# A fused depthwise convolution, MLP and gate on one core: the last 16 channels in eight PSUM banks, a reordered first product group, and image 2's forms on VectorE

## The chip, the cores and the metric

The kernel runs on one core of a Trainium2 chip. TensorE multiplies matrices into PSUM; VectorE (DVE), ScalarE (ACT) and GpSimd (POOL) work elementwise; SyncE (SP) mostly issues transfers. The metric is the device time of one execution in microseconds. Everything is float32.

## The reference, cut to what matters

The input is 32 images of 384 channels and 28 x 28 pixels.

```python
residual = x                                               # (32, 384, 28, 28)
y = conv(x, dw_w, padding=3, groups=384) + dw_b            # depthwise, 7 x 7
y = to_nhwc(y)
mu, var = mean(y, -1), mean((y - mu) ** 2, -1)             # over the channels of a pixel
y = (y - mu) * rsqrt(var + 1e-6) * ln_g + ln_b
y = gelu(y @ w1 + b1)                                      # 384 -> 1536
gx = sqrt(sum(y ** 2, pixels))                             # per image and channel
nx = gx / (mean(gx, -1) + 1e-6)
y = grn_g * (y * nx) + grn_b + y
x = residual + to_nchw(y @ w2 + b2)                        # 1536 -> 384
# gate: mean, max and min over the pixels of each channel, small products
logits = concat(avg @ W1.T, maxes * W2_2, min @ W3.T) @ Wfc.T
out = sigmoid(logits[:, :, None, None] + x)
```

The statistics of a pixel need all 384 channels. No image can therefore be normalized before the convolution of the last channel is done.

## The kernel before, in words

**Stage 1, the convolution.** Images lie in 8 groups of 4; a transfer `load_x` brings 32 channels of one group. `pad_x` copies it to a padded tile (POOL line 479, ACT line 481), and `turn_x` transposes it on TensorE (line 491) and copies it out of PSUM into `xt`. The first eight (padding, transposes) run one after the other before the first product. The 7 x 7 filter becomes banded 128 x 128 matrices `tmat`, loaded by `load_t` from the DRAM tables `fs`, which are built from `dw_w`. The channels go in 48 groups of 8 (s = 0 to 47). `conv` does two channels at a time: three matmuls each (lines 696, 698, 700), a transpose on VectorE (line 703) into `yt`, a sum over channels into `acc` (line 711), squares on ACT (line 717) and their sum into `ssum` on POOL (line 727). `yt` is stored to `yd` in DRAM. During these groups `form_w` (lines 556 to 573) writes combinations of w1 and w2 to `u1d` and `u2d`.

**The last 16 channels.** Groups 46 and 47 are done in two halves, first images 0 to 15, then 16 to 31, on four PSUM banks in turn (`pcs`). After the first half, image 0's last channels are read back (`load_y_part`), and its statistics are formed by `finish` in tiles (`late_tiles`) that lie where an `xt` tile was: sums, a VectorE reduction of the four partial square sums (line 746), a root on ACT (line 753), a reciprocal (line 754) and a store to `rsd[0]`; then the same for the other half into `rsd[1]`.

**Image 0.** `first_image` makes the raw image (line 789 VectorE, line 792 ACT), and `forms_up` the ten FORMS (line 358): sums and differences of channel blocks and pixel halves, named p to z. Since the first linear layer needs no statistics apart from a scale per pixel, image 0's products start on raw data, and `stretch` (line 952) multiplies the outputs by that scale afterwards. Later images are normalized first: `normed` (line 315) takes the loaded image `yi` and the broadcast scale `rb`.

**Stage 2, per image.** `up(b)` computes the first linear layer as four tiles t, in two pairs; each pair runs through 15 UPSTEPS, one matmul a tile and step (line 986, 128 x 392), so 60 in all. Results collect in banks A, B and C of a tile and are taken out by ACT copies (line 993) and VectorE sums (lines 997 to 1005). Weights come in groups of five steps by `load_u1` into six buffers in `ws`. `down(b)` computes the second layer in 38 STEPS of three matmuls (line 1116, 128 x 196) in banks A to I, whose operands are made by 39 SUMS on POOL (`sums`, line 1077); VectorE adds the products to the residual (lines 1132, 1134) and takes max and min (line 1143). Between them lie `gelu` (line 945), `square` into `junk` (line 958), `grn` (lines 1008 to 1025, with the one-column product `pg`), `scale` (lines 324 VectorE, 326 ACT) and `gate_store` (line 1160 on, with the product `pa` and its reading into `lt`).

**The order.** The driver runs up(0), up(1), down(0), up(2), down(1), up(3) and so on. `within(b)` and `beside(b)` are tables of hooks: at step (pair, matmul) of `up`, or at step i of `down`, they issue the elementwise work of neighbouring images. Instructions pinned by `keep_in_program_order` stay as written; the rest is ordered by a scheduler. All loads of stage 2 go through SP's queue. Every PSUM tile of stage 2 comes from one pool of eight buffers:

```python
    psz = ctx.enter_context(tc.tile_pool(name="psz", bufs=8, space=bass.MemoryType.PSUM))

    def bank(name):
        return psz.tile([P, 512], F32, tag="pz", name=name)
```

Of the kernel before, what the change touches and what calls it, by code (L numbers as in the profile page):

```python
# [13 lines left out]
P = 128  # L14
# [72 lines left out]
)  # L87
NS = len(UPSTEPS)
KT = FB // 3
# [108 lines left out]
def convnext_gate_kernel(  # L198
# [24 lines left out]
    rsd = [dram.tile([P, YR], F32, name=f"rsd_{i}") for i in range(2)]  # L223
# [18 lines left out]
    fct = const.tile([P, CB, NQ, R], F32, name="fct")  # L242
    eps_t = const.tile([P, 1], F32, name="eps_t")
# [9 lines left out]
    def load_u1(t, i):  # L253
        n = len(u1_tiles) % NU1
        w = ws[:, n * UG * P : (n + 1) * UG * P].rearrange("p (g c) -> p g c", c=P)
        nc.sync.dma_start(w, u1d[t, :, i : i + UG, :])
        u1_tiles.append(w)
        return w
# [12 lines left out]
    last_u2 = []  # L271
    B0 = min(B, 16)

    def load_y(b):
        yi = yis[b] = yip.tile([P, CB, NQD, YR], F32, tag="yi", name=f"yi_{b}")

        with tc.issue_after(last_u2[-1]) if last_u2 else ExitStack():
            for cb in range(CB):
                load_y_part(b, yi, cb, 0, P)
        load_rb(b)  # L280

    def load_rb(b):
        if b == 0:
            rb = d_room[:, : NQD * YR].rearrange("p (q n) -> p q n", n=YR)
        else:
            rb = rbp.tile([P, NQD, YR], F32, tag="rb", name=f"rb_{b}")
        rbs[b] = rb
        base = rsd[0 if b < B0 else 1]
        nc.sync.dma_start(
            rb,  # L290
            bass.AP(
                tensor=base.tensor,
                offset=base.offset + b * YR,
                ap=[[0, P], [B * YR, NQD], [1, YR]],
            ),
        )

    def load_y_part(b, yi, cb, p0, p1):
        nc.sync.dma_start(
# [8 lines left out]
    def normed(b, cbs=range(CB)):  # L308
# [5 lines left out]
        for cb in cbs:  # L314
# [4 lines left out]
            if b == 1:  # L319
# [8 lines left out]
    def forms_up(b, eng=nc.gpsimd, early=None):  # L328

        if b in feats:  # L330
            o, af = feats[b], early_af.pop()
            make_forms(b, eng, o, af, [d for d in FORMS if d[0] not in EARLY])
            return
        acc = accs.pop(b)
        o = feats[b] = {
            f"{k}{'ab'[h]}": acc[:, k, h * NH : (h + 1) * NH] for k in range(CB) for h in range(2)
        }
        ns = len(FORMS) - 1
        if b == 1:

            n = -(-ns * NH // (KD * NQ4))
            reserved.extend(slots[SLOTS - n :])
            del slots[SLOTS - n :]
            aft = d_room[:, (SLOTS - n) * KD * NQ4 :]
            af = [aft[:, n * NH : (n + 1) * NH] for n in range(ns)]
        else:
            af = [room_af[:, n, :] for n in range(ns)]
        if early:
            early_af.append(af)
        make_forms(b, eng, o, af, [d for d in FORMS if not early or d[0] in EARLY])  # L350

    EARLY, early_af = ("q", "t", "u"), []

    def make_forms(b, eng, o, af, todo):
        places = [d[0] for d in FORMS if d[0] != "w"]
        for name, place, in0, in1, op in todo:
            d = o[place] if name == "w" else af[places.index(name)]
# [4 lines left out]
    with ExitStack() as one:  # L362
# [8 lines left out]
        finp = one.enter_context(tc.tile_pool(name="finp", bufs=1))  # L371
# [18 lines left out]

        dww = scratch([CB, 49])
        nc.sync.dma_start(dww, dw_w.rearrange("(cb p) t -> p cb t", p=P))
# [49 lines left out]
        NX = C // XC  # L442
        NG = B // NB
        NXI = 8
        xi_last = tp.tile([P, NT], F32, name="xi_last")
        ssum = finp.tile([P, SQ, YR], F32, name="ssum")
        acc = finp.tile([P, 2, N], F32, name="acc")
        dws = finp.tile([P, 1], F32, name="dws")
        lr = tp.tile([P, CB, 2], F32, name="lr")
        mcol = tp.tile([P, FB], F32, name="mcol")  # L450
        for t in (ssum, acc):
            nc.gpsimd.memset(t, 0.0)
        GT = NX * NG
        xis = {}

        def load_x(i):

            k, g = divmod(i, NG)
            n = i % NXI
            t = xis[i] = xi_last if n == NXI - 1 else room[:, n * NT : (n + 1) * NT]  # L460
            base = x[g * NB, k * XC : k * XC + 1, :]
            nc.sync.dma_start(
                t,
                bass.AP(
# [817 lines left out]
    if B > 1:  # L1282
        load_y(1)
# [49 lines left out]
```

## Time and profile before

| what | us |
|---|---|
| median of three runs | 3053.81 (3052.74 to 3055.58) |
| the profiled execution | 3053.83 |
| its span | 3052.1 |
| TensorE busy in the span | 2998.0 |
| convolution ends, `up(0)` begins | 498.6, 504.85 |
| `up(1)` begins, `pg` of image 0 | 558.66, 582.47 |
| `down(0)` begins, ends | 604.64, 650.84 |
| from image to image afterwards | 78.2 |

Times inside the span start at its first instruction. The page gives busy time of each engine over the span; the windows give the same for stretches of it; the timeline lists what an engine did, with the idle time ahead of a line and what ended it. TensorE's own clock can be lowered: the windows list the share that was granted.

### The profile page before, as it was taken

Reading aid. Unit: us, or ns where it says so; the run is one execution under the profiler, and the core shown is the slowest. Engines: PE = TensorE matmul, PEld = TensorE weight load, DVE = VectorE, ACT = ScalarE, POOL = GpSimd, SP = SyncE. Lnnn points to the kernel's source line nnn. Section 1 sums busy time; section 2 is a strip of 40 time slices with the busy share of each in tenths; the row PEclk is TensorE's granted clock in tenths of the full one; section 3 lists DMA queues with packets and bytes.
Section 4 is the critical chain, followed back from the end, with each engine's and each line's share of the span. In section 5 each row is a group of like instructions: output and inputs, shape, how many; then the busy total and the mean of one; then the engine's idle time right before and its main releaser. Section 6 shows DMA issues by size and latency. Waiting matters only on the chain.

```text
span 3052.1 us, 43990 instructions
## 1 busy us (share of the span) xinstructions
PE 2998.0 (98%) x14436; PEld 2426.9 (80%) x14436; DVE 2042.5 (67%) x4643; ACT 1794.6 (59%) x2919; POOL 2444.9 (80%) x1819
## 2 busy tenths in 40 slices
PE   8999998999999999999999999999999999999998
PEld 8999996577777777777777777777777777777777
DVE  6767667756666666666666666666666666666665
ACT  4455553746666666666666666666666666666661
POOL 3457874699888888888888888888888888888897
PEclk9999999999999999999999999999999999999999
DMA  9899997445666566666666566666566566666545
GB/s 368 327 354 381 363 339 232 141 161 199 205 206 202 202 206 206 198 206 206 201 202 202 190 201 206 200 197 195 195 197 198 197 201 203 201 201 201 195 152 197
DMA packets 279369, 674.15 MB, mean 221 GB/s; under 512 B 24346, under 2 KB 99944, under 8 KB 273128
## 3 DMA queue, kind: packets, MB, share of 16 engines
q1 hardware_dynamic: 266456, 633.37, 61.6%
q10 hardware_dynamic: 12688, 37.97, 3.2%
q8 instruction: 118, 1.93, 0.2%
q14 instruction: 107, 0.88, 0.1%
HBM read 575.57 MB, written 95.68 MB: 220 GB/s over the span
## 4 chain that ended last, share of the span: by engine, by line
PE 89%; POOL 5%; DVE 4%; issue 1%; ACT 1%; DMA 1%; SPq 0%; DVEq 0%; ACTq 0%; POOLq 0%
PE ph_C L986 13%; PE ph_A L986 12%; PE ph_B L986 11%; PE pz_A L1116 8%; PE pz_C L1116 8%; PE pz_F L1116 7%; PE pz_D L1116 7%; PE pc L696 5%; PE pc L698 4%; PE pc L700 4%; PE pt L491 2%; PE pz_H L1116 2%; PE pz_I L1116 2%; PE pz_E L1116 2%; POOL d_room L1077 2%; DVE room L315 2%
## 5 line engine op out<-in xcount | busy, mean ns | idle before, releaser
L326 ACT ACTIVATE y<-y,vecs,gsc 128x784 f32<-128x784 f32 x372 | 359.1, 1031 | 463.9 <-DVE gsc L1024 463.9
L1077 POOL TENSOR_TENSOR d_room<-y 128x588 f32<-128x588 f32 x253 | 364.7, 1443 | 287.8 <-PE pz_B L1116 192.1
L945 ACT ACTIVATE y<-y,b1f 128x784 f32<-128x784 f32 x384 | 350.5, 945 | 209.1 <-DVE y L1003 179.0
L986 PE MATMUL ph_B<-room,ws 128*128 128x392 f32 x1240 | 461.7, 495 | 10.5 <-issue 6.0
L986 PE MATMUL ph_C<-room,ws 128*128 128x392 f32 x1240 | 462.0, 495 | 7.3 <-DVE y L1001 4.6
L986 PE MATMUL ph_A<-room,ws 128*128 128x392 f32 x1240 | 459.0, 492 | 3.4 <-ACT te L993 1.8
L1077 POOL TENSOR_TENSOR d_room<-d_room,y 128x588 f32<-128x588 f32 x308 | 441.3, 1437 | 16.8
L986 PEld LDWEIGHTS ph_C<-room,ws 128*128 128x128 f32 x1240 | 233.3, 190 | 191.3 <-DVE y L1001 28.7
L986 PEld LDWEIGHTS ph_A<-room,ws 128*128 128x128 f32 x1240 | 235.4, 190 | 177.0 <-ACT te L993 2.4
L986 PEld LDWEIGHTS ph_B<-room,ws 128*128 128x128 f32 x1240 | 235.6, 191 | 175.7 <-issue 6.8
L727 POOL TENSOR_TENSOR ssum<-ssum,sq 128x896 f32<-128x896 f32 x96 | 200.8, 2092 | 168.5 <-ACT sq L717 167.0
L958 ACT ACTIVATE junk<-y 128x784 f32<-128x784 f32 x384 | 329.1, 857 | 9.0
L1077 POOL TENSOR_TENSOR d_room<-y,d_room 128x588 f32<-128x588 f32 x214 | 306.4, 1438 | 26.7 <-PE pz_D L1116 15.7
L358 POOL TENSOR_TENSOR room<-room 128x392 f32<-128x392 f32 x303 | 303.9, 1020 | 11.9
L717 ACT ACTIVATE sq<-yt,dwb 128x224 f32<-128x224 f32 x376 | 160.4, 474 | 225.1 <-DVE yt L703 213.0
L1077 POOL TENSOR_TENSOR y<-y 128x588 f32<-128x588 f32 x180 | 259.0, 1439 | 7.1
L999 DVE TENSOR_TENSOR y<-y,ph_B 128x392 f32<-128x392 f32 x256 | 137.4, 557 | 158.3 <-ACT y L945 123.4
L997 DVE TENSOR_TENSOR y<-y,ph_C 128x392 f32<-128x392 f32 x384 | 213.1, 562 | 25.2
L703 DVE STREAM_TRANSPOSE yt<-pc 128x448 f32<-128x448 f32 x184 | 119.4, 649 | 136.9 <-PE pc L700 100.3
L1116 PE MATMUL pz_A<-d_room,u 128*128 128x196 f32 x1050 | 203.7, 330 | 0.1
L696 PE MATMUL pc<-xt,tmat 128*128 128x224 f32 x736 | 200.2, 354 | 0.6 <-ACT xt L502 0.6
L1116 PEld LDWEIGHTS pz_A<-d_room,u 128*128 128x128 f32 x1050 | 179.7, 191 | 7.7 <-POOL d_room L1077 0.4
(266 smaller groups left out, 6375.7 us busy)
## 6 DMA issues: line engine op xcount, KB each, us to landing
u<-u2d SPq DMA_DIRECT2D x487, 384.0 KB, 3.7
ws<-u1d SPq DMA_DIRECT2D x384, 320.0 KB, 3.0
tmat<-fs SPq DMA_DIRECT2D x47, 1420.0 KB, 10.8
ws<-u2d SPq DMA_DIRECT2D x121, 384.0 KB, 3.9
yi<-yd SPq DMA_DIRECT2D x95, 448.0 KB, 6.3
yd<-yt SPq DMA_DIRECT2D x47, 896.0 KB, 6.8
x<-in_x SPq DMA_DIRECT2D x32, 1176.0 KB, 5.6
out<-x ACTq DMA_DIRECT2D x31, 1176.0 KB, 9.6
```

The lines of the kernel that those rows point to most:

```text
L326: eng.activation(out, in_, AF.Identity, bias=add, scale=mul)
L358: tc.keep_in_program_order(eng.tensor_tensor(d, o[in0], o[in1], op))
L696: keep(nc.tensor.matmul(po, t[:, c, P : 2 * P], xc, start=True, stop=False))
L717: nc.scalar.activation(sq[:, cy % SQ + ci], yt[:, cy + ci], AF.Square, bias=dwb[:, cc + ci : cc + ci + 1], scale=1.0,)
L727: nc.gpsimd.tensor_tensor(to, base, sq, ALU.add)
L945: ins = nc.scalar.activation(y, y, AF.Gelu, bias=b1f[:, f : f + 1], scale=1.0)
L958: ins = nc.scalar.activation(junk, ys[b][:, f, :], AF.Square, accum_out=ssqs[b][:, f : f + 1])
L986: nc.tensor.matmul(banks[t, bk][:, :NH], wts[t][:, i % UG, :], o[opnd], start=(first == 1), stop=True, skip_group_check=True,)
L997: nc.vector.tensor_tensor(d, d, p, ALU.add)
L999: nc.vector.tensor_tensor(d, d, p, ALU.subtract)
L1077: nc.gpsimd.tensor_tensor(d[0], o[a][0], o[c][0], ALU.add if sign == "+" else ALU.subtract)
L1116: nc.tensor.matmul(pz[:, :NQ4], wt[:, i % UD, t, :], o[opnd][0][:, t, :], start=(first and t == 0), stop=(t == KD - 1), skip_group_check=True,
```

## The change

At the start, the image loads are issued before the load of `dw_w`, which becomes the third, and the pads run three image groups ahead of the transposes.

For the last 16 channels, eight PSUM banks (three of the transposes, one of the weight preparation, four of the convolution) hold one pair of channels each, and are filled by the two halves of images in turn. The first half only transposes its products out; sums and squares are taken once, over all images, in the second half. There is one `finish`, cut into four parts: part 0 (two POOL additions of the partial square sums, then forms v, x, z) before `up(0)`, and parts 1 to 3 from hooks in its first pair. `acc` and `ssum` move to a tile `stats` that stays; `rsd` is one tile.

The raw third block of image 0 is all ACT's. Its forms are POOL's: q, t, u, w early, p, r, s during the second half, v, x, z in part 0. The first pair of tiles of `up(0)` takes its steps in the order FIRST_UP, with a fourth bank D. The weights of the second pair, groups 0 and 1, are loaded early into four of the u2 buffers.

PSUM of stage 2 comes from two pools of four, taken in turn by four tiles. The two y buffers have a pool each, so that y_0 no longer lies over the tiles of the statistics; `junk` goes, and squares are written to `stats` or `room`.

Hooks of the first images move: `normed(1)`, forms and loads of image 2 go into the second pair of `up(0)`, stretches are all POOL's, half of image 0's later squares and five of its twelve scales are VectorE's, three of its sums (s1, s5, s6) too, and image 2's ten forms run on VectorE during `down(0)`.

The core of the diff ("..." marks what is left out):

```diff
+FIRST_UP = (
+    ("w", "A", 1, (("A", "copy", "E"),)),
+    ("1a", "B", 1, (("B", "rsub", "E"),)),
+    ("0b", "A", 0, (("A", "negated", "1b"),)),
+    ("0a", "B", 0, (("B", "negated", "0a"),)),
+    ("t", "C", 1, (("C", "add", "E"),)),
+    ("q", "A", 0, (("A", "plus", "0b"),)),
+    ("u", "B", 0, (("B", "minus", "1a"),)),
+    ("p", "D", 1, (("D", "copy", "2b"),)),
+    ("s", "C", 1, (("C", "add", "0a"),)),
+    ("x", "A", 1, (("A", "copy", "2a"),)),
+    ("r", "D", 0, (("D", "sub", "2a"), ("D", "sub", "0a"), ("D", "add", "0b"))),
+    ("2a", "C", 0, (("C", "add", "2a"),)),
+    ("v", "A", 0, (("A", "sub", "2b"), ("A", "sub", "1b"), ("A", "add", "1a"))),
+    ("z", "C", 1, (("C", "add", "2b"), ("C", "add", "1b"))),
+    ("2b", "D", 1, (("D", "add", "2b"),)),
+)
...
+PLACE = {step[0]: i for i, step in enumerate(UPSTEPS)}
...
-    rsd = [dram.tile([P, YR], F32, name=f"rsd_{i}") for i in range(2)]
+    rsd = dram.tile([P, YR], F32, name="rsd")
...
+    stats = const.tile([P, SQ * YR + 2 * NJ * B], F32, name="stats")
+    ssum = stats[:, : SQ * YR].rearrange("p (c n) -> p c n", n=YR)
+    acc = stats[:, SQ * YR :].rearrange("p (c n) -> p c n", c=2)
...
-        dww = scratch([CB, 49])
-        nc.sync.dma_start(dww, dw_w.rearrange("(cb p) t -> p cb t", p=P))
...
+        LENT = (3, 5, 7)
+        AHEAD = B // NB
...
+        dww = scratch([CB, 49])
+        for i in range(AHEAD):
+            load_x(i)
+            if i == 1:
+                nc.sync.dma_start(dww, dw_w.rearrange("(cb p) t -> p cb t", p=P))
...
-        for i in range(AHEAD):
-            load_x(i)
+        for i in range(NPAD):
+            pad_x(i)
         xt = new_xt(0)
         for i in range(NG):
-            pad_x(i)
...
+            if i + NPAD < NG:
+                pad_x(i + NPAD)
...
-                pc = pcs.pop(0)
-                pcs.append(pc)
+                pc = pcs[(s - NK + 2) * PAIRS + c2]
...
+            if b1 < B:
+                return
+            keep(nc.vector.tensor_tensor(acc, acc, pc[:, :, :N], ALU.add))
...
-                to, base = ssum, ssum
-                if nb < B and not b0:
-                    to = late["s2"]
-                    base = ssum if s == NK - 2 and cy < SQ else to
-                nc.gpsimd.tensor_tensor(to, base, sq, ALU.add)
+                ins = nc.gpsimd.tensor_tensor(ssum, ssum, sq, ALU.add)
+                if s >= NK - 2:
+                    keep(ins)
...
+                for i in range(2 * PAIRS):
+                    if i < 3:
+                        pc = psx.tile([P, 4, P], F32, tag="pt", name=f"pc_x{i}")
+                    elif i == 3:
+                        pc = psb.tile([P, 4, P], F32, tag="pb", name="pc_b")
+                    else:
+                        pc = psc.tile([P, 2, 256], F32, tag="pc", name=f"pc_c{i}")
+                    if i < 4:
+                        pc = pc.rearrange("p a b -> p (a b)").rearrange("p (c m) -> p c m", c=2)
+                    pcs.append(pc)
+                    if B0 < B:
+                        nc.vector.memset(
+                            pc[:, :, :N].rearrange("p c (j b) -> p c j b", b=B)[:, :, :, B0:],
+                            0.0,
+                        )
+                for i in (UG, 2 * UG, 0):
+                    for t in range(2):
+                        first_u1[t, i // UG] = load_u1(t, i)
...
-                            if not half:
-                                nc.sync.dma_start(yd[:, ch, :], y2[i])
-                            else:
-                                for q in range(NQD):
-                                    (nc.sync, nc.scalar)[q % 2].dma_start(
-                                        yd[q * B + b0 : q * B + b1, ch, :],
-                                        y2[i][q * B + b0 : q * B + b1],
-                                    )
+                            keep(nc.sync.dma_start(yd[:, ch, :], y2[i]))
+                        if b1 == B and n == PAIRS:
+                            first_image(2)
+                        if b1 == B and n == PAIRS + 1:
...
-    psz = ctx.enter_context(tc.tile_pool(name="psz", bufs=8, space=bass.MemoryType.PSUM))
+    pszs = [
+        ctx.enter_context(tc.tile_pool(name=f"psz{i}", bufs=4, space=bass.MemoryType.PSUM))
+        for i in range(2)
+    ]
+    nbanks = 0
 
     def bank(name):
-        return psz.tile([P, 512], F32, tag="pz", name=name)
+        nonlocal nbanks
+        nbanks += 1
+        return pszs[(nbanks - 1) // 4 % 2].tile([P, 512], F32, tag="pz", name=name)
...
+            steps = [(x[0],) + x[2:] for x in UPSTEPS]
+            if b == 0 and t2 == 0:
+                steps = FIRST_UP
+            for i, (opnd, bk, first, acts) in enumerate(steps):
                 for t in (t2, t2 + 1):
-                    if i % UG == 0:
-                        wts[t] = first_u1.pop((t, i), None) or load_u1(t, i)
+                    g, gi = divmod(PLACE[opnd], UG)
+                    if (t, g) not in wts:
+                        wts[t, g] = first_u1.pop((t, g), None) or load_u1(t, g * UG, b <= 1)
                     if i == 0:
...
+    def finish(part):
+
+        keep = tc.keep_in_program_order
+        tmp = yis[0].rearrange("p k q n -> p (k q n)")
+        mu0, s1, mu, va, s2, rs = (tmp[:, i * YR : (i + 1) * YR] for i in range(6))
+        if part == 1:
+            keep(nc.vector.tensor_tensor(mu0, acc[:, 0], acc[:, 1], ALU.add))
+            keep(nc.vector.transpose(s1, mu0))
+            keep(nc.vector.tensor_scalar(mu, s1, dws, 1.0 / C, ALU.add, ALU.mult))
+            keep(nc.vector.tensor_tensor(va, mu, mu, ALU.mult))
+        elif part == 0:
+            for n in (SQ // 2, 1):
+                to = ssum[:, :n] if n > 1 else s2.unsqueeze(1)
+                keep(nc.gpsimd.tensor_tensor(to, ssum[:, :n], ssum[:, n : 2 * n], ALU.add))
+            forms_up(0, ("v", "x", "z"))
+        elif part == 2:
+            keep(nc.vector.scalar_tensor_tensor(va, s2, 1.0 / C, va, ALU.mult, ALU.subtract))
+            keep(nc.vector.tensor_scalar(va, va, 0.0, EPS, ALU.max, ALU.add))
+            keep(nc.scalar.activation(s2, va, AF.Sqrt))
+        else:
+            keep(nc.vector.reciprocal(rs, s2))
+            keep(nc.sync.dma_start(rsd, rs))
+            load_rb(0)
+            if B > 1:
+                load_y(1)
...
+    LENT_SUMS = ("s1", "s5", "s6")
...
+            eng = nc.vector if b == 0 and name in LENT_SUMS else nc.gpsimd
...
+            at((0, 3), finish, 1)
+            at((0, 13), finish, 2)
+            at((0, 17), finish, 3)
+            for i, m in enumerate(first_outs[:HF]):
+                at((0, 29), stretch, m, nc.gpsimd)
+                at((2, 5 + 4 * i), gelu, b, m)
+                at((2, 7 + 4 * i), square, b, m)
             if B > 1:
-                at((0, 20), normed, 1)
-                at((0, 24), forms_up, 1)
-            for m in range(HF):
-                at((2, 4 * m), stretch, m, nc.gpsimd)
+                for cb in range(CB):
+                    at((2, 7 + 4 * cb), normed, 1, (cb,))
+                at((2, 16), forms_up, 1)
             if B > 2:
-                at((2, 0), load_y, 2)
+                at((2, 20), load_y, 2)
         elif b == 1:
-            for m in range(HF):
-                at((0, 2 * m), stretch, HF + m, (V, nc.gpsimd)[m % 2])
-                at((0, 6 + 2 * m), gelu, p, HF + m)
-                at((0, 17 + m), square, p, HF + m)
-            at((0, 23), grn, p)
+            for i, m in enumerate(first_outs[HF:]):
+                at((0, 2 * i), stretch, m, nc.gpsimd)
+                at((0, 6 + 3 * i), gelu, p, m)
+                if i % 2:
+                    at((0, 8 + 3 * i), square, p, m)
+                else:
+                    at((0, 11 + 3 * i), square, p, m, V)
+            at((0, 29), grn, p)
             for i, f in enumerate(order):
-                at((0, 24) if i < 6 else (2, 0), scale, p, f, V if i % 3 else A)
-            at((0, 26), sums, p)
-            at((2, 0), sums, p)
-            at((2, 12), sums, p)
+                at((2, 2 + i), scale, p, f, V if i in (1, 3, 5, 8, 11) else A)
+            for i in range(4, 30, 2):
+                at((2, i), sums, p)
...
-            at("after sums", forms_up, b + 2)
+            if b == 0:
+                for i, d in enumerate(FORMS):
+                    at(12 + 2 * i, forms_up, 2, (d[0],), V)
+            else:
+                at("after sums", forms_up, b + 2)
...
+    for g in EARLY_G:
+        for t in (2, 3):
+            w = u2_tiles[2 * g + t - 2][:, : UG * P].rearrange("p (g c) -> p g c", c=P)
+            tc.keep_in_program_order(
+                nc.sync.dma_start(w, u1d[t, :, g * UG : (g + 1) * UG, :])
+            )
+            first_u1[t, g] = w
+    finish(0)
     up(0, within(0))
     load_x(0)
```

## The prediction

> **What bounds the kernel now.** I read the page's busy shares first, then the chain that ended last, then the busy time by stage, then the idle times of TensorE in order of time.
>
> ```profile
> span 3052.1 us, 43990 instructions
> PE 2998.0 (98%) x14436; PEld 2426.9 (80%) x14436; DVE 2042.5 (67%) x4643; ACT 1794.6 (59%) x2919; POOL 2444.9 (80%) x1819
> PE 89%; POOL 5%; DVE 4%; issue 1%; ACT 1%; DMA 1%; SPq 0%; DVEq 0%; ACTq 0%; POOLq 0%
> ```
>
> TensorE is busy for 98% and carries 89% of the chain. No other engine can be the bound over the whole span; only TensorE's 54 us of idleness, and what it runs at a lower clock, can be won. The busy time by stage says where these lie:
>
> ```profile
> core 0: us, PE busy (x) PEld busy (x) DVE busy (x) ACT busy (x) POOL busy (x), PEclk, DMA share, GB/s
> 0.00:25.00 25.00, 13.74 (x85) 11.79 (x86) 9.64 (x20) 10.67 (x18) 7.16 (x21) 1.00 0.92 348
> 500.00:550.00 50.00, 35.82 (x97) 19.42 (x98) 33.37 (x56) 13.71 (x27) 18.99 (x15) 0.90 0.70 205
> 620.00:640.00 20.00, 16.52 (x85) 15.23 (x84) 8.94 (x25) 4.47 (x5) 19.45 (x14) 0.91 0.39 120
> 760.00:3000.00 2240.00, 2234.42 (x10129) 1752.34 (x10128) 1497.75 (x3563) 1383.72 (x2138) 1903.36 (x1433) 1.00 0.61 200
> 3000.00:3053.00 53.00, 39.22 (x221) 37.69 (x219) 27.10 (x99) 5.25 (x6) 32.92 (x26) 0.92 0.48 158
> ```
>
> Columns: window, length, busy time of each engine, granted clock. Idle TensorE: 11.3 us at the start, 14.2 between 500 and 550, 3.5 in the first `down`, only 5.6 in 2240 us of steady state, 13.8 at the end. The timeline of TensorE names the stalls of the transition; the last line is ScalarE's:
>
> ```profile
> 504.85 2.95 PE L986 MATMUL ph_B<-room,ws 128*128 128x392 f32 x4 [6.04 <-issue]
> 518.54 2.98 PE L986 MATMUL ph_B<-room,ws 128*128 128x392 f32 x4 [4.43 <-ACT y L993]
> 582.47 0.38 PE L1016 MATMUL pg<-gs,ones_f 128*128 128x1 f32 x2 [2.13 <-DVE gs L1014]
> 624.17 1.26 PE L1116 MATMUL pz_E<-y,u 128*128 128x196 f32 x6 [1.66 <-POOL y L1077]
> 634.14 2.24 PE L1116 MATMUL pz_H<-d_room,u 128*128 128x196 f32 x6 [1.52 <-POOL d_room L1077]
> 517.99 0.89 ACT L993 ACTIVATE y<-ph_B 128x392 f32<-128x392 f32 x2 [8.41 <-DMA rsd<-xt]
> ```
>
> Columns: start, length, work, and in brackets the idle time ahead and its releaser. The convolution ends at 498.6, `up(0)` begins at 504.85 after the forms, stops at 514.1 because ScalarE's first eviction waits for the store of the statistics, and `down(0)` ends at 650.84, held by POOL's `sums`.
>
> **What the Trainium skill says.** "TensorE: Matmul & The Clock Gate", What's actually happening: the clock is granted by recent activity, about 3.4 us of work bring it back. The trace agrees: after the two long waits four matmuls took 2.95 and 2.98 us, where four otherwise take 1.48. "SBUF — State Buffer", Who interferes with whom: a VectorE operation on two SBUF inputs and a POOL operation that reads SBUF exclude each other. The trace agrees: `normed` (line 315, 784 columns) took 0.97 us each in the three at 531, and 2.10 beside POOL's stretches at 550. "Perfetto Trace Analysis", Matmuls: matmul groups should rotate through PSUM banks so that eviction overlaps the next group. That is what the split into two pools of four touches; before, TensorE lost nothing to it in steady state.
>
> **The change part by part**, in the time base of the kernel before, against its profiled 3053.83 us (median of the runs 3053.81, so the two are one).
>
> *Start.* The first image loads are issued ahead of the `dw_w` load and the pads run three groups ahead, so the three ACT waits of 1.32 us between transposes go; the transposes could end near 17. The convolution then waits for the first half of `tmat_0` (8.5 us before); its source, the `fs` store, needs `dw_w`, which is now the third load, about 1 us later: first product near 17.8 instead of 20.42, a gain of 2.6. `tmat_1` (10.2 us, issued behind it) is then late: needed at 28.1, landing near 28.9, minus 0.9. Net 1.7; bounds 0 (all of it waits for `tmat`) and 3.
>
> *Last 16 channels.* Eight banks take away the one wait of 0.47 us on `acc` at 488.53; the first half loses 8 sums of 0.3 us on VectorE, 16 squares and 4 POOL adds, none on TensorE's path. Gain 0.5: convolution ends at 498.1.
>
> *Start of `up(0)`.* The reordered first group begins with w, 1a, 0b, 0a, t, q, u, which need only channel blocks 0 and 1 of the raw image, there by 498. So the 6.04 us go. Then 0b waits about 1.1 us, because ACT's copies of the w products sit behind the last squares (0.42 each) and the raw block. The y tiles no longer overlay the statistics, so the 4.43 go too, and with them 2 x 1.5 us of slow clock. A pair of tiles is 15 steps of two matmuls (1.32 us a step): 30 x 0.658 = 19.7. With 1.1 and 0.8 for the later forms, p, r, s and v, x, z, on POOL (1.02 each) the first pair ends near 519.7.
>
> *Statistics.* Two POOL adds replace two VectorE reductions of 1.7 us. Folds end near 508.7, the root and reciprocal (1.55) near 513.2, the store lands 3 us later, the broadcast of rs for image 0 near 521.7, image 1's loads near 525. Stretches (1.94 each) run 521.8 to 533.5, `normed(1)` 525 to 531, or to 534 if it contends with them. forms(1) start near 534, as before.
>
> *Second pair of `up(0)`.* 19.7 of matmuls. Groups 0 and 1 of the weights are early, in the u2 buffers. Group 2 of t=3 is an ordinary load; on SP's queue it stands behind image 2's three loads and its broadcast, and these wait for the buffers that `normed(1)` frees. Issue near 533 to 536, 7.8 us to land behind such loads: TensorE stalls 3.5 us and then runs slow for 1.4. Another 1.8 us go to evictions on VectorE queued behind `normed`. End near 546.1.
>
> *`up(1)`, then `down(0)`.* Half of `up(1)`, 19.7, and 2 us of waits as seen there before: pg near 567.8 instead of 582.47, so 14.7 earlier. After pg, `down(0)` hangs on POOL: ACT's and VectorE's scales let s2 start at +9.2; three sums moved to VectorE leave 28 up to s31, at 1.46 each 40.9; s31 releases the last 15 steps, 15 x 0.995 plus waits, 16.7. End at pg + 66.8 = 634.6; before 582.47 + 68.4 = 650.84. So 16.2 earlier. TensorE's own work would allow about 620.
>
> *Image 2's forms on VectorE.* They run under `down(0)`'s products, 10 x 0.5 us; POOL's 10.4 us at 644.5 go, and a wait of 0.36 us at 654.
>
> *Steady state.* Same instructions. But two pools of four change who shares a bank. In most images the new neighbour was read well before: F of `down`, read last (at 2217.37 when `up` began at 2215.09), is wanted again by the fifth matmul at 2217.72, 0.25 us to spare. In one image of four, from image 2 on, the gate's bank `pa` takes the bank of D, and its matmul and the first I step move near the end of `down`. VectorE then reads I behind a max and a min (0.92 each), the second I step waits some 0.3 us, and the evictions of the next `up` begin about 1.2 us later, past a slack near 1.2. I take 0.5 us for each of 7 images, 3.5 us of loss; bounds 0 and 8.
>
> The end (13.8 us idle) has nothing changed in it. **Sum:** 1.7 + 0.5 + 16.2 + 0.4 - 3.5 = 15.3; 3053.8 - 15.3 = 3038.5, taken as 3038.
>
> **The rivals.** *TensorE-bound:* the weights of the second pair arrive in time and the sums keep ahead, as the early groups and three sums on VectorE suggest; against it, POOL was 19.45 of 20 us busy in 620 to 640. `down(0)` would end near 623, 11 us earlier than I say: 3027. *Queue:* image 2's loads hold SP longer, since `normed(1)` contends with the stretches (2.62 at worst in 550 to 566), group 2 of both tiles of the pair comes late, and pg falls near 575: 7 us of the gain lost, 3045. *No gain in the sums:* pg earlier, but VectorE's forms and sums exclude POOL's, each sum 2.0 instead of 1.46: 28 x 0.54 = 15, all of it; the start and forms remain, less the bank waits: 3052. *Slower:* the bank of F in every image. If VectorE reads F a microsecond later than before, the fifth matmul waits 0.75 us, and evictions behind it as much again; over 31 images, at 1 us each, 31 us against a gain of 18.8: 3066. It decides from 0.6 us per image; for it speaks the slack of 0.25, against it that VectorE's work ahead of F is the same.
>
> **How the numbers follow.** Likeliest case 0.45, TensorE-bound 0.17, queue 0.22, no gain in the sums 0.08, slower 0.08. A measurement tells about 0.2%, 6 us, from no change. The likeliest runs from 3032 to 3044. The range 3025 to 3050 holds the first three and leaves out most of the last two and the edge of the second. Faster: 0.45 + 0.17 and 0.16 of the queue case, 0.78; same 0.13; slower 0.09.
>
> **What would show it.** Right: the first product near 17.8; `up(0)` begins within a microsecond of the convolution's end, with no wait for the statistics' store; a wait in its second pair for weights from u1d; pg near 568; `down(0)` waiting for line 1102's sums, ending near 635; and TensorE idle from 760 on near 9 instead of 5.6, in every fourth image. Wrong: a wait for a bank in each image, a `down(0)` with no wait for POOL (then nearer 3027), or pg later than 575 (nearer 3045).

## The result, and the profile after

The kernel after takes 3040.47 us, the median of five runs (3039.83 to 3041.86); the kernel before, run beside it on the same chip, takes 3055.58. The ratio is 0.9951, its 95% interval 0.9936 to 0.9966: faster by half a per cent. The forecast was 3038. The profiled execution took 3041.33, 12.5 less than that of before. The times of kernels are medians; one execution of one experiment, the kernel without early weights, took 6430.47 us, twice the others, and is in no ratio.

The page of the kernel after, its span, busy time and chain:

```profile
span 3039.6 us, 43826 instructions
...
PE 2996.2 (99%) x14436; PEld 2427.9 (80%) x14436; DVE 2036.2 (67%) x4643; ACT 1787.4 (59%) x2899; POOL 2431.9 (80%) x1811
...
PE 91%; POOL 3%; DVE 3%; DMA 2%; issue 1%; ACT 1%; SPq 0%; ACTq 0%; DVEq 0%; POOLq 0%
```

TensorE does the same matmuls in the same time. It is idle for 43 us instead of 54. POOL's share of the chain falls from 5 to 3%; DMA's rises from 1 to 2%, a first sign of new waits. A product of stage 2 stands twice on a timeline, so x4 is one step of two tiles; where the text counts four matmuls in a line, as the prediction does, it counts these entries. The busy time by stage of the kernel after (window, length, busy time of each engine, granted clock, DMA):

```profile
core 0: us, PE busy (x) PEld busy (x) DVE busy (x) ACT busy (x) POOL busy (x), PEclk, DMA share, GB/s
0.00:25.00 25.00, 14.91 (x81) 12.85 (x82) 9.54 (x20) 10.52 (x18) 7.10 (x20) 0.97 0.84 295
500.00:550.00 50.00, 43.14 (x124) 23.60 (x123) 35.94 (x60) 24.17 (x47) 33.84 (x26) 0.97 0.68 233
600.00:620.00 20.00, 15.71 (x78) 14.28 (x79) 11.22 (x25) 3.40 (x6) 19.61 (x14) 0.91 0.46 146
620.00:640.00 20.00, 18.39 (x109) 17.90 (x108) 17.28 (x46) 11.35 (x13) 19.30 (x14) 1.00 0.73 242
760.00:2990.00 2230.00, 2220.74 (x10072) 1742.02 (x10071) 1482.19 (x3546) 1374.53 (x2125) 1893.96 (x1432) 1.00 0.61 200
2990.00:3042.00 52.00, 40.22 (x232) 39.77 (x232) 25.68 (x96) 5.25 (x6) 30.42 (x24) 0.90 0.46 156
```

Between 500 and 550 TensorE is busy 43.1 us instead of 35.8: the gain lies there. In the first 25 us, where a gain was expected, it has done 81 matmuls, and 85 before. In `down(0)` (600 to 620 here, 620 to 640 before) POOL is as full as it was, 19.6 of 20. The timeline of TensorE names the waits that are left:

```profile
17.69 0.65 PE L718 MATMUL pc<-xt,tmat 128*128 128x224 f32 x2 [0.58 <-ACT xt L527]
...
22.53 0.98 PE L516 MATMUL pt<-ident,xpad 128*128 128x128 f32 x7 [2.52 <-ACT xpad L506]
...
530.91 1.84 PE L979 MATMUL ph_C<-room,u 128*128 128x392 f32 x4 [2.87 <-DVE y L992]
532.55 2.82 PE L979 MATMUL ph_A<-ws,u 128*128 128x392 f32 x4
...
543.68 1.56 PE L979 MATMUL ph_B<-d_room,ws 128*128 128x392 f32 x4 [1.59 <-ACT y L988]
547.49 0.93 PE L979 MATMUL ph_B<-room,ws 128*128 128x392 f32 x2 [2.25 <-DMA ws<-u1d]
...
570.52 0.28 PE L1039 MATMUL pg<-gs,ones_f 128*128 128x1 f32 x2
...
613.32 1.68 PE L1139 MATMUL pz_E<-y,u 128*128 128x196 f32 x6 [2.06 <-POOL y L1102]
...
624.00 1.26 PE L1139 MATMUL pz_H<-d_room,u 128*128 128x196 f32 x6 [1.61 <-POOL d_room L1102]
```

The 6.04 and 4.43 us around the start of `up(0)` are gone. In their place stand three waits in its second pair (2.87, 1.59, 2.25) and four matmuls at 2.82 behind the first of them. `down(0)` still hangs on line 1102's sums.

By the starts of TensorE's stages in the two traces, the 12.4 us between the last gate products of the two came about so:

| stretch | before | after | change | forecast |
|---|---|---|---|---|
| start to first product of the last 16 channels | 477.88 | 479.57 | +1.7 | -1.7 |
| from there to `up(0)` | 26.97 | 20.05 | -6.9 | |
| `up(0)` to `pg` | 77.62 | 70.90 | -6.7 | |
| the last two together | 104.59 | 90.95 | -13.6 | -14.7 |
| `pg` to `up(2)` (end of `down(0)`) | 68.37 | 68.51 | +0.1 | -1.6 |
| `up(2)` to `up(31)` | 2268.01 | 2267.27 | -0.7 | +3.1 |
| `up(31)` to the last gate product | 125.59 | 125.72 | +0.1 | 0 |

The forecast's last 0.5 is a slip: the last channels' 0.5 is in the 14.7 already and was added once more. So the number came out well in part by luck, because errors of both signs met: 3.4 lost at the start, 1.1 in the transition, 1.7 in `down(0)`, 0.5 by the slip, and 3.8 won back in the steady state.

### The profile page after: what moved, and what is told of

Read it like the earlier page. It is cut to its first block, busy times and chain, and to the rows that moved or that the text cites. A ratio compares the mean times of both kernels' runs of the same rounds, so it can differ in the third digit from the quotient of the medians.

```text
span 3039.6 us, 43826 instructions
## 1 busy us (share of the span) xinstructions
PE 2996.2 (99%) x14436; PEld 2427.9 (80%) x14436; DVE 2036.2 (67%) x4643; ACT 1787.4 (59%) x2899; POOL 2431.9 (80%) x1811
## 4 chain that ended last, share of the span: by engine, by line
PE 91%; POOL 3%; DVE 3%; DMA 2%; issue 1%; ACT 1%; SPq 0%; ACTq 0%; DVEq 0%; POOLq 0%
PE ph_C L979 13%; PE ph_A L979 12%; PE ph_B L979 12%; PE pz_A L1139 8%; PE pz_C L1139 8%; PE pz_D L1139 7%; PE pz_F L1139 7%; PE pc L718 5%; PE pc L720 4%; PE pc L722 4%; PE pt L516 2%; PE pz_H L1139 2%; PE pz_I L1139 2%; POOL d_room L1102 2%; PE pz_E L1139 2%; DVE room L344 1%
## 5 line engine op out<-in xcount | busy, mean ns | idle before, releaser
L1102 POOL TENSOR_TENSOR d_room<-d_room,y 128x588 f32<-128x588 f32 x308 | 442.8, 1442 | 16.7
L979 PE MATMUL ph_B<-room,ws 128*128 128x392 f32 x1220 | 451.7, 492 | 2.3 <-DMA ws<-u1d 2.3
L979 PEld LDWEIGHTS ph_C<-room,ws 128*128 128x128 f32 x1224 | 230.6, 190 | 182.2 <-DVE y L996 21.7
L741 POOL TENSOR_TENSOR stats<-stats,sq 128x896 f32<-128x896 f32 x96 | 200.8, 2092 | 176.6 <-ACT sq L735 175.9
L947 ACT ACTIVATE stats<-y 128x784 f32<-128x784 f32 x381 | 326.7, 858 | 9.1
```

Of the source, the lines that this page charges most:

```text
L741: ins = nc.gpsimd.tensor_tensor(ssum, ssum, sq, ALU.add)
L947: ins = nc.scalar.activation(stats[:, :NT], ys[b][:, f, :], AF.Square, accum_out=ssqs[b][:, f : f + 1])
L979: ins = nc.tensor.matmul(banks[t, bk][:, :NH], wts[t, g][:, gi, :], o[opnd], start=(first == 1), stop=True, skip_group_check=True,)
L1102: eng.tensor_tensor(d[0], o[a][0], o[c][0], ALU.add if sign == "+" else ALU.subtract)
```

## The experiments

Each is the kernel after with one edit, unless it says otherwise. A ratio is to the kernel before that ran beside the experiment; that kernel's median was 3055.6 us beside the kernel after and 3057.3, 3058.9 and 3060.9 beside the experiments, so the times of two experiments can differ by more than an edit is worth. By their intervals, only the kernel with both repairs and its variant with `normed(1)` later lie apart from the kernel after. What a single part is worth is read from the stages of the traces, one trace each.

**The start: `dw_w` first again.**

```diff
+        nc.sync.dma_start(dww, dw_w.rearrange("(cb p) t -> p cb t", p=P))
         for i in range(AHEAD):
             load_x(i)
-            if i == 1:
-                nc.sync.dma_start(dww, dw_w.rearrange("(cb p) t -> p cb t", p=P))
```

> The changed kernel with one line moved back: the dw_w load is issued before the image loads, the pads stay three groups ahead. My theory: the third place cost 4.3 us on everything behind the fs store (first half of tmat_0 issued at 13.06 instead of 8.05, the next image loads at 14.44 instead of 10.10), and so the wait of 2.52 us at 22.53 and 1.5 us of slow clock after it. Then the first product stays near 17.7 to 18.5, the wait for the pad at 22.5 goes, and the first half product of the last channels, at 479.57 in the changed kernel, comes at 475.5 to 477.5; the time falls by 2 to 4 us to about 3037. Rival: the start is bound by the transfers' sum, and what is won ahead is lost at tmat_1; then that product stays at 479 to 480 and the time within 1 us of 3040.5.

Measured: 3038.98 us (ratio to before 0.9941, 0.9927 to 0.9956); first product at 16.45, first product of the last channels at 476.63. The chain of waits (start, length, what) in the kernel after begins with these transfers:

```profile
2.13 5.02 DMA scr<-in_dw_w
...
14.44 7.10 DMA room<-in_x
```

and in the experiment:

```profile
0.81 2.07 DMA scr<-in_dw_w
...
9.63 9.48 DMA room<-in_x
```

Behind two image loads the small load takes 5.02 us instead of 2.07 and starts 1.3 later. All that hangs on it moves by as much: the `fs` store is issued at 7.54 (3.29 before), and as it sits on ACT's own queue, ACT's first copy of `xt` waits too (9.89, 7.86 before); the `tmat` loads start at 13.06 (8.05 before), and the next images' loads behind them on SP's queue at 14.44 (10.10). TensorE in the experiment:

```profile
16.45 0.65 PE L717 MATMUL pc<-xt,tmat 128*128 128x224 f32 x2 [0.58 <-ACT xt L526]
...
20.10 0.98 PE L515 MATMUL pt<-ident,xpad 128*128 128x128 f32 x7 [1.32 <-ACT xpad L505]
```

The next channels' transposes start at 20.10; in the kernel after at 22.53, at 22.58 before. So the lead of 2.7 us at the first product was eaten by the late images within 5 us, and after that wait the products from 23.35 to 26.60 ran at little over half speed (0.79 to 0.95 a pair, where the experiment has 0.49 to 0.55).

One trace is not enough for a size here. Over the eight kernels with the changed start, the first product of the last channels lies between 477.16 and 479.57, mean 478.2; over the four with `dw_w` first and pads ahead, between 476.47 and 476.74; the one trace of before has 477.88. The late `dw_w` costs about 1.6; pads ahead win about 1.3, measured against the one trace of before; the two together come to nothing that can be told apart.

**The old start whole** (the edit above, and `pad_x(i)` back inside the loop).

> The changed kernel with the start of the kernel before: dw_w loaded first, each pad just ahead of its transposes. The first product then comes near 20.4 (before 20.42) and the first half product of the last channels near 477.9 (before 477.88). With the changed start, eight looks at the same code (the changed kernel and seven of the kernels here) gave 477.2 to 479.6 for the latter, mean 478.2; with dw_w first and pads ahead one look gave 476.6. Theory: the pads ahead alone win 1.3 us and the later dw_w load gives 1.5 back, so the start as changed is worth nothing; this kernel is within 1 us of the changed one. Rival (the prediction's step): the changed start is worth 1.7, and this kernel's last channels begin near 479.9.

Measured: 3042.24 (ratio 0.9944, 0.9929 to 0.9959), against 0.9951 for the kernel after: no difference. Its profiled execution took 7 us more than its other runs, with slower transposes at the start (14 in 3.25 us three times; the kernel before has 3.25 once and 1.99 twice) and the first product at 24.66, so its trace says nothing on the point. Inconclusive by itself; the mean above carries the reading.

**One PSUM pool of eight instead of two of four.**

```diff
-        ctx.enter_context(tc.tile_pool(name=f"psz{i}", bufs=4, space=bass.MemoryType.PSUM))
-        for i in range(2)
+        ctx.enter_context(tc.tile_pool(name=f"psz{i}", bufs=8, space=bass.MemoryType.PSUM))
+        for i in range(1)
...
-        return pszs[(nbanks - 1) // 4 % 2].tile([P, 512], F32, tag="pz", name=name)
+        return pszs[0].tile([P, 512], F32, tag="pz", name=name)
```

> The changed kernel with all stage-2 PSUM tiles from one pool of eight again. The prediction's step (two pools cost 3.5 us in steady state) expects TensorE's stage from up(2) to up(31) shorter by 3 to 4 us than the 2267.3 us of the changed kernel. My theory after its trace: no bank wait shows there, and the split removes a wait of 0.2 us behind normed in one image of four, so one pool gives 2268 (as the kernel before had, 2268.0), up to 1 us slower, and the transition within 1 us.

Measured: 3042.69 (ratio 0.9951, 0.9936 to 0.9966), the ratio of the kernel after; `up(2)` to `up(31)` takes 2267.30, and 2267.27 with two pools. TensorE's waits from 760 to 2990 (total, how often, longest), in the kernel after:

```profile
PE pz_A L1139 <- DMA ws<-u2d: 4.3, 1, 4.3
PE ph_C L979 <- DVE y L996: 2.9, 12, 0.8
```

and with one pool:

```profile
PE ph_C L979 <- DVE y L996: 2.9, 17, 0.2
```

The waits for C are within one tile: the step t writes C anew and waits until VectorE has read that same C, in both kernels alike (before, 4.0 in all). A wait of more than 0.2 us for a bank that another tile held is in neither. In ten other kernels with two pools `up(2)` to `up(31)` took 2265.7 to 2267.3 (the one with POOL's forms, below, left out), so two pools may win up to 1.6 there; they lose nothing there. The place where the loss was expected can be looked at: as image 4's `up` begins, the eviction of B, VectorE's reading of that bank, comes 4.91 us after the start of `up` in the kernel after as in that before, though VectorE ends the reductions 0.31 later than before. It had 0.67 to spare.

The 4.3 is one wait in `down(31)`, and it comes from the two pools. The chain of waits of the kernel after runs through it:

```profile
2981.26 1.12 PE pz_I L1139 x6
2982.41 7.41 DMA ws<-u2d
2989.96 2.30 PE pz_A L1139 x6
```

The forecast had the first product into I move to the end of `down` in one image of four. It did: it is the 35th of the 38 steps instead of the 29th in images 2, 6 and so on to 26, the 34th in image 30, and with one pool it never moves. That product holds a weights buffer until 2982.4. The next load into this buffer, the first weights of `down(31)`, is issued right after, and TensorE waits 4.26 for it. After the other images an `up` comes before the next `down`, and no such wait shows there. The kernel with the old order of steps, below, is a second test: it has two pools, but its first pair takes two banks fewer, the product moves in images 4, 8 and so on to 28, and the wait isn't there. All eleven kernels with two pools and FIRST_UP have it (3.5 to 5.4). How much of it is lost stays open: the stage from `up(31)` took 125.1 to 127.8 in these eleven and 121.9 with the old order, but 123.8 with one pool and 125.6 before, both with waits of 1.63 and 1.78 for POOL in `down(31)` instead.

With one pool the transition was longer (a wait of 1.94 for the sums of line 729 at the start of `up(0)`; `up(0)` to `pg` 72.55 instead of 70.90).

**The old order of steps in the first pair.**

```diff
-            if b == 0 and t2 == 0:
-                steps = FIRST_UP
```

> The changed kernel with the first pair of tiles of up(0) in the old order of steps (p, s, x first), three banks a tile; all else stays. If the new order is what let TensorE go straight on from the convolution (499.4 to 499.6), the third step waits for form x on POOL, which ended at 512.9: TensorE stalls 9 to 11 us between 501 and 513, and pg moves from 570.5 to 578 to 582; the time rises 7 to 11 us to 3048 to 3051. Rival: the chain through the statistics, image 1's normalization and its forms sets pg whatever the order; then pg moves by under 3 us and the time by under 3.

Measured: 3049.8 (ratio 0.9973, 0.9962 to 0.9984); `up(0)` to `pg` 80.75. TensorE waits twice for POOL's forms, and runs slow after each:

```profile
502.37 2.98 PE L977 MATMUL ph_B<-room,ws 128*128 128x392 f32 x4 [4.51 <-POOL room L386]
...
510.51 2.98 PE L977 MATMUL ph_A<-room,ws 128*128 128x392 f32 x4 [3.76 <-POOL room L386]
```

From the first product of the last channels to `pg` it takes 105.5 us instead of 90.95, and 104.59 before: the transition's gain is all gone. The whole time rises by less, 9.3 us (6.7 by the ratio), since in these traces the start is 1.9 shorter and the stage from `up(31)` 3.9. The reordered first group is worth the most of the single parts, by this and the runs below.

**No early weights for the second pair.**

```diff
-    EARLY_G = (0, 1)
+    EARLY_G = ()
```

> The changed kernel without the early weights: groups 0 and 1 of the second pair are loaded into the six ordinary buffers when these come free. My theory: they come free only as the first pair runs its last steps, and SP is then busy with image 1's loads, so the second pair waits for weights at its begin, 3 to 6 us more than the 2.25 in the changed kernel; pg moves by 3 to 6 us and the time rises by as much. Rival: the stretches and normed hold the second pair anyway; then under 1 us.

Measured: 3047.47 (ratio 0.9962, 0.9946 to 0.9978), `up(0)` to `pg` 80.10. One wait, at the second pair's first matmul:

```profile
527.21 2.98 PE L979 MATMUL ph_B<-room,ws 128*128 128x392 f32 x4 [8.32 <-DMA ws<-u1d]
```

More than expected, since the first of these loads is issued at 518.04, behind the three loads and the broadcast of image 1, and lands 9.12 later. From the first product of the last channels to `pg` it takes 100.1 us, 4.4 less than before. So of the 13.6 us won in the transition the order of steps alone keeps 4.4, and the early weights alone keep nothing: the two are needed together.

**Image 2's loads two steps later.** This tests the queue step of the forecast.

```diff
-                at((2, 20), load_y, 2)
+                at((2, 22), load_y, 2)
```

> The changed kernel with image 2's loads two hooks later in the second pair of up(0), so that the weights of group 2 for both tiles go ahead of them on SP's queue. The prediction's step: the wait for these weights (2.25 us in the changed kernel at 547.49) goes, pg comes 2 to 2.5 us sooner and the time falls by 2 to 2.5 us. Rival: TensorE then waits for image 1's forms on POOL instead (they end at 547.1), and pg moves by under 1 us.

Measured: 3036.44 (ratio 0.9931, 0.9916 to 0.9946); `up(0)` to `pg` 67.44, 3.5 less than in the kernel after. SP's queue in the kernel after:

```profile
522.64 2.82 SPq L279 DMA_DIRECT2D ws<-u1d  x3
536.64 1.47 SPq L328 DMA_DIRECT2D yi<-yd  x3
538.16 0.51 SPq L316 DMA_DIRECT2D rb<-rsd  x1
538.71 1.31 SPq L279 DMA_DIRECT2D ws<-u1d  x2
```

SP stands still from 525.5 to 536.6, since image 2's load can't go before the last `normed(1)`, which ends at 536.6, has freed its buffer; the weights behind it are issued at 538.71 and reach TensorE at 547.49. In the experiment one weight load more is issued ahead of image 2's. The waits of 1.59 and 2.25 are gone. The expectation had only the second; the first, for ACT's copies of B, went too, and the scheduler no longer puts steps of `up(1)` between those of the second pair, so what the 1.59 hung on isn't told apart. Only this stays in the second pair:

```profile
529.49 2.03 PE L979 MATMUL ph_C<-room,u 128*128 128x392 f32 x4 [2.89 <-DVE y L992]
531.31 2.77 PE L979 MATMUL ph_A<-ws,u 128*128 128x392 f32 x4
```

Its cause is on VectorE, in the kernel after:

```profile
528.09 2.30 DVE L344 SCALAR_TENSOR_TENSOR acc<-yi,vecs,rb 128x784 f32<-128x784 f32 x1 [2.01 <-DMA rb<-rsd]
530.31 1.02 DVE L992 TENSOR_TENSOR y<-y,ph_C 128x392 f32<-128x392 f32 x2
```

`normed(1)` waits for the broadcast of the scale, and takes 2.30 beside POOL's stretches (the last of its three, at 535.59, takes 1.02); the evictions of C, ready by then, wait behind it.

**Image 2's forms on POOL, after the sums, as before.**

```diff
-            if b == 0:
-                for i, d in enumerate(FORMS):
-                    at(12 + 2 * i, forms_up, 2, (d[0],), V)
-            else:
-                at("after sums", forms_up, b + 2)
+            at("after sums", forms_up, b + 2)
```

> The changed kernel with image 2's ten forms back on POOL after its sums. In the changed kernel the second half of down(0) waits for POOL (H at 624.0, 53.5 us after pg) and single sums there took 1.6 to 1.75 us beside VectorE's forms instead of 1.44. My theory: the forms on VectorE cost POOL about 1 us up to H, and save the 10.4 us behind the sums; without them H comes about 1 us sooner after pg, and up(2) begins sooner by as much, but waits up to 1 us for its forms: time within 1.5 us of the changed kernel. Rival (the prediction's step): forms on VectorE are free, H does not move and up(2) loses 0.4 us.

Measured: 3043.07 (ratio 0.9953, 0.9938 to 0.9968). H, the first product after the last long wait in `down(0)`, comes 52.40 after `pg` instead of 53.48; but `up(2)` then waits:

```profile
642.01 1.58 PE L979 MATMUL ph_A<-room,ws 128*128 128x392 f32 x4 [2.01 <-POOL room L386]
```

So the forms on VectorE win 2.0 and lose 1.1: they aren't free, as the forecast had them, since they take 1.08 us each in `down(0)` on average (0.68 to 1.80), not 0.5, and POOL's sums beside them take longer.

**The three sums back on POOL, and ten on VectorE.**

```diff
-    LENT_SUMS = ("s1", "s5", "s6")
+    LENT_SUMS = ()
```

> The changed kernel with s1, s5 and s6 of image 0 back on POOL. The prediction's step: each sum on POOL is 1.46 us of the chain that sets the end of down(0), so H comes 3 x 1.46 = 4.4 us later after pg (57.9 instead of 53.5) and the time rises by 4.4. Rival: since the two engines exclude each other on these sums, a sum moved to VectorE still blocks POOL for its 0.72 us or longer, and s2 has to wait for s1; then H moves by 1 to 2.5 us only.

Measured: 3044.47 (ratio 0.9957, 0.9943 to 0.9971); H at `pg` + 56.35, 2.9 later, between the two expectations. A sum taken from POOL wins 0.96, not the 1.46 of the forecast.

```diff
-    LENT_SUMS = ("s1", "s5", "s6")
+    LENT_SUMS = ("s1", "s5", "s6", "s7", "s8", "s10", "s15", "s23", "s26", "s30")
```

> The changed kernel with seven more sums of image 0 on VectorE (s7, s8, s10, s15, s23, s26, s30 beside s1, s5, s6). If POOL's sums set the end of down(0), each of the seven that comes before s31 takes 1.44 us off POOL; where VectorE runs beside POOL half of it is given back (0.72 us a sum): H comes 4 to 8 us sooner after pg, up(2) too, and the time falls by 4 to 8 us to 3033 to 3037. Rival: VectorE, with image 2's forms and normalization and the products' additions in its queue, is the next bound; then the additions come late, TensorE waits for banks in down(0), and the gain is under 2 us.

Measured: 3041.25 (ratio 0.9947, 0.9932 to 0.9962); H at `pg` + 54.54, no gain. VectorE takes up s23 and stands. The operands of s23 don't come from POOL, but it writes to a place that POOL's s22 reads last, and it starts as s22 ends:

```profile
602.89 0.77 DVE L1102 TENSOR_TENSOR y<-y 128x588 f32<-128x588 f32 x1 [7.11 <-POOL y L1102]
603.58 0.35 DVE L1155 TENSOR_TENSOR x<-x,pz_D 128x196 f32<-128x196 f32 x1
```

Behind it waits the eviction of D, and TensorE, whose next product goes into D, stands 5.66 us, until 604.03.

**Both repairs together** (`dw_w` first, image 2's loads two steps later).

> The changed kernel with both repairs: dw_w loaded first (one look gave 1.5 us off), image 2's loads two hooks later (3.4 us off between the begin of up(0) and pg). They lie in different stages, so they should add: pg near 477 + 20.1 + 67.4 = 564.5, up(2) near 633, time near 3035 (between 3033.5 and 3036.5). Rival: the loads of the start vary by 2 us from one execution to the next whatever the order; then the median is that of the queue alone, 3036.4.

Measured: 3034.02 (3033.5 to 3034.76; ratio 0.9913, 0.9899 to 0.9926), faster than either kernel. `pg` is at 564.00 and `up(2)` at 632.57, 6.5 earlier each than in the kernel after: the two effects add.

Two attempts to go on from there brought nothing. `normed(1)` at later steps:

```diff
-                    at((2, 7 + 4 * cb), normed, 1, (cb,))
+                    at((2, 9 + 3 * cb), normed, 1, (cb,))
```

> Both repairs, and the normalization of image 1 two to zero hooks later in the second pair of up(0) (hooks 9, 12, 15 instead of 7, 11, 15), so that the first evictions of the second pair aren't queued behind it. If the wait of 2.9 us at 530.91 (second C step behind normed, which waits for the broadcast of rs) is TensorE's own loss, it goes and pg comes 2 to 3 us sooner than with the two repairs alone. Rival: image 1's forms on POOL, which begin after normed, set the begin of up(1); then a wait of 2 to 3 us appears there and pg moves by under 1 us.

Measured: 3035.37 (ratio 0.9916, 0.9902 to 0.993); `pg` 0.9 earlier, the wait of 2.88 becomes two of 1.64 and 0.88 for VectorE, and one of 0.88 for weights is new. And with that, s23, s26 and s30 on VectorE beside s1, s5 and s6:

> The same with s23, s26 and s30 on VectorE beside s1, s5, s6: three sums from the middle of down(0), where VectorE's queue is shorter than in up(1), in which the seven more sums brought waits of 1.0 and 1.6 us. By the measured worth of a moved sum (2.9 us for three) H comes 2 to 3 us sooner after pg than 53.5. Rival: VectorE blocks on the inputs or the places of these sums as it did with seven (5.66 us lost at 604), and H comes no sooner.

Measured: 3037.94 (ratio 0.9925, 0.9912 to 0.9939), H at `pg` + 58.2. VectorE once more, at s23 again:

```profile
600.27 0.77 DVE L1101 TENSOR_TENSOR y<-y 128x588 f32<-128x588 f32 x1 [15.93 <-POOL y L1101]
```

with TensorE waiting 11.48 us for the evictions behind it.

## Why the prediction was right, and where it was wrong

**Start: wrong, no gain.** The first product came at 17.69 for a forecast of 17.8, but not as argued: it waited for ACT's last copy of `xt`, not for `tmat`. The step that failed is "now the third load, about 1 us later". The `fs` store came 4.25 later, and the step counted the late load's effect on `tmat` alone. It left out what else stands behind it: the next images on SP's queue, and ACT's copies behind the store. The forecast took a gain at one point, the first product, for a gain of the stage. Part of the 3.4 is chance: the trace has the latest start of the eight with the same code, and their mean, 478.2, is 2.0 behind the forecast.

**Last 16 channels and the start of `up(0)`: right.** 0.7 for 0.5, and the convolution's last product is followed by `up(0)` after 0.22 us, with no wait for the statistics. The first pair took 20.6 us from the convolution's last product (forecast 21.6), the two matmuls of the second pair that the scheduler put into it left out; of the waits of 1.1 and 0.8 that the forecast allowed, under 1 us came. The old order brings two waits of 4.51 and 3.76 back.

**Second pair: right in mechanism, 2.5 long.** It took 28.9 us instead of 26.4, eight matmuls of `up(1)` that lie in it left out. The queue step held: SP stood behind image 2's loads, and taking that away won 3.5 where the step had 4.9. The term too small was "1.8 us ... evictions on VectorE queued behind `normed`": 2.87 of wait, and some 1.8 more at the slow clock. After the wait four matmuls took 2.82 instead of 1.48, as the Trainium skill has it ("TensorE: Matmul & The Clock Gate", What's actually happening). After the same wait, 2.85, in the one-pool kernel the next four took 1.58 and then 1.48, so a wait of this length lowers the clock in some traces and not in others. `up(1)`'s half took 21.6 (forecast 21.7).

**`down(0)`: right in mechanism, 1.7 long.** s2 started at `pg` + 9.1 (forecast 9.2). But the 28 sums up to s31 took 44.3 us, 1.58 each, instead of 40.9. POOL in the kernel after:

```profile
597.00 1.43 POOL L1102 TENSOR_TENSOR d_room<-y,d_room 128x588 f32<-128x588 f32 x1
598.40 2.17 POOL L1102 TENSOR_TENSOR d_room<-d_room,y 128x588 f32<-128x588 f32 x1
...
622.32 1.63 POOL L1102 TENSOR_TENSOR d_room<-d_room 128x588 f32<-128x588 f32 x1
623.91 1.74 POOL L1102 TENSOR_TENSOR y<-y,d_room 128x588 f32<-128x588 f32 x1
```

The sum of 2.17 lies beside a `normed` of image 2 on VectorE, those of 1.63 and 1.74 beside forms of image 2; by itself a sum takes 1.43. This is the exclusion that the Trainium skill states ("SBUF — State Buffer", Who interferes with whom), which the forecast quoted for `normed` beside stretches and applied here only in a rival (8 in 100), at 2.0 a sum. Beside VectorE's additions that take a product from PSUM, as at 590.57, a sum stays at 1.44. The truth lay between, nearer the likeliest case. After s31 it went faster than forecast, 15.1 instead of 16.7, so 1.7 in all.

**Image 2's forms: 0.4 forecast, some 0.9 measured** (2.0 less 1.1).

**Steady state: wrong in size and place.** From `up(2)` to `up(31)` nothing was lost. The term that failed is "the evictions of the next `up` begin about 1.2 us later, past a slack near 1.2": the reductions end 0.31 later, within a slack of 0.67, and the evictions come at the same 4.91. The product into I did move in every fourth image, as forecast, but what that cost came by way of a weights buffer, once, in `down(31)`. The sign that was to show it, TensorE idle near 9 us, did come (9.3), but not in every fourth image: 4.3 of it is this one wait. A total can agree while its parts don't.

**The rivals.** TensorE-bound (3027) fails by the waits for sums. The queue case (3045) had the right wait at a third of the size. No gain in the sums: its own terms (15.3 less 15.1) come to 3053.6, not 3052; the sums took 1.58, not 2.0. Banks of F in every image: no such wait in the trace.

## What to carry to other kernels

A load that is moved is paid by everything behind it on its queue and by everything that its result is needed for; follow both before a gain at the first product is booked. Before work goes from a full engine to a free one, price it beside the other engine's work (of three sums two thirds of their time were won), and place it where its operands are ready and the place that it writes to is free: VectorE, waiting, held all evictions behind it. A new sharing of banks can change the order of steps, and with it when other buffers come free. A wait is sometimes repaired by two steps in an issue order, as with image 2's loads.

## What had not been expected of the hardware

The same start code came to its last channels between 477.16 and 479.57 in eight kernels, a spread of 2.4 us, as large as the effects that were forecast there; in four with `dw_w` first the spread was 0.3. A 73.5 KB load behind two of 392 KB took 5.02 us where it takes 2.07 first. The Trainium skill says that VectorE is a strict FIFO ("Perfetto Trace Analysis", Tensor Engine Instruction (MATMUL, LD_WEIGHTS)), and the traces agree at a higher price than expected: one instruction waiting for POOL held VectorE for 7.11 and 15.93 us.
